# An S5 block and an SLN attention on one Trainium2 core: the closing layernorm split into halves, its product with g on GpSimd, later key loads, and seam values by way of ScalarE

## The chip, the cores and the metric

The kernel runs on one core of one Trainium2 chip. The metric is the device time of one launch in microseconds (us). The core has five engines that run their own instruction streams in program order: TensorE (PE, matrix products; PEld is its weight load), VectorE (DVE), ScalarE (ACT), GpSimd (POOL) and SyncE (SP, which here issues every DMA transfer). Engines wait for each other on semaphores.

## The reference

The input is x of shape (2, 2048, 512) and a condition vector per batch element. A first part, the S5 block, is a layernorm, a linear recurrence over time, and a gated feed-forward with GELU. Its output `hidden` goes through attention with a conditioned layernorm (SLN) on both sides:

```python
def _sln(h, w, ln_g, ln_b, Wg, bg, Wb, bb):
    mu = jnp.mean(h, axis=-1, keepdims=True)
    var = jnp.mean((h - mu) ** 2, axis=-1, keepdims=True)
    ln = (h - mu) / jnp.sqrt(var + EPS) * ln_g + ln_b
    gamma = (w @ Wg.T + bg)[:, None, :]
    beta = (w @ Wb.T + bb)[:, None, :]
    return gamma * ln + beta
h = _sln(hidden, w, ln_g, ln_b, Wg, bg, Wb, bb)
qkv = (h @ Wqkv.T + bqkv).reshape(B, N, num_heads, hd, 3)
...
att = jax.nn.softmax(energy, axis=-1) / D ** 0.5
out = jnp.einsum('bhqk,bhkd->bhqd', att, v)
...
out = out @ Wp.T + bp
h1 = out + hidden
h2 = _sln(h1, w, ln_g, ln_b, Wg, bg, Wb, bb)
return h2 + h1
```

There are 16 heads of 32, and every query sees all 2048 keys. The change lies in the last two lines (the second SLN, called the last norm below), in when keys and values are loaded, and in how some of the values v are written.

## The kernel before, in words

**Stages.** From 0 to 1380 us the S5 block and the feed-forward run in chunks of 512 tokens. The seam, to 1487 us, is where the last chunk's norm, features, heads and values (`at_norm`, `at_features`, `at_heads`, `at_values`) alternate with the first steps of attention. Attention runs to 3514 us, and the last four tiles are closed by `end_last` at 3551 us.

**Blocks and periods.** Attention is 64 blocks, one for each batch element b, pair of heads p and chunk c of 512 queries; batch element 0 has blocks 0 to 31, batch element 1 has 32 to 63. A block lasts 8 periods, called p0 to p7 here. The main loop (`for j in range(FIRST, NP * N + 2)`) writes one period after another, and an engine runs its instructions in the order written. Two blocks are under way in each period: for the block 15 periods ahead (AHEAD) scores and maxima are computed, for the block of now the exponentials and the weighted sum.

**One period, in the order written.** First `run_due(j)` issues what the dictionary `due` holds for j: loads, transposes, closing steps. Then, for the block of now, `make` (L812) computes a score tile again: PE writes `s` (L751), DVE adds the shift and writes `pT` (L816). For the block ahead, `across` (L769) has PE compute `m` (L776) and DVE reduce it to `top` (L781). `exponentials` on ACT (L821) follows. `keep` (L758) has PE compute a score tile, ACT copy it into a ring (L762) and DVE take the running maximum `run` (L767). Then comes the period's second exponential, `take_off` on POOL (L810, score minus maximum, for the next period) and `weighted` on PE (L831, o). Of 16 key tiles, ten are kept and six made anew.

**From the maxima to the shift.** `turn_run` (L783) transposes the running maximum on PE into the bank `pt_run` (L787) and DVE reduces it (L788); it comes twice, at a block's p2 for the one head and p4 for the other. `spread` at p5 transposes the result (`pt_neg`), copies it on ACT, and sends it through DRAM: SP writes `flat` (L802) and reads it back broadcast as `shift` (L804), 512 KB. POOL's `take_off` of the block waits for `shift`.

**One PSUM bank for many.** The scores `s` have two buffers of two banks, `m` two banks, `o` one. The bank with the tag "pt" is shared by `pt_run`, `pt_neg`, the projection `py`, the norm's `dev` and `z`: each has to wait until the one before it was read for the last time.

**Loads.** `load_k` reads 8 x 256 KB for the pair that opens at block n, every fourth block, and is due at period 8n - 27, which is p5 of block n - 4, ahead of that period's `spread`. `load_q` (8 transfers) is due at p3, `load_v` at 8n - 9, but not before OPEN, four periods ahead of block 0.

**Closing.** The 16 query tiles of batch element 0 are closed in blocks 34 to 56, those of the first three chunks of batch element 1 (12 tiles) in blocks 60 to 63. For a tile of batch element 0, with k at a block's p3: `fetch` at k (L874: the sums' quotients `by`, o and the residual `xr`), `divide` on POOL at k + 2, `project` in four matmuls at k + 3 to k + 6 (p6, p7, p0, p1) with `moments` (L909, DVE) right behind the last one, `deviation` (L917, eleven small DVE operations, the inverse root by Newton steps) at k + 7 (p2), `last_norm` at k + 8 (p3: ACT writes `z`, L941; DVE multiplies it by g, L943) and `close` at k + 9 (p4: two adds on POOL, L949 and L950, and the store). All of these are run by `run_due` at the start of their period.

Of the kernel before, what the change touches and what calls it, by code (L numbers as in the profile page):

```python
# [19 lines left out]
P = 128  # L20
# [19 lines left out]
def tile_s5_block_then_sln_attention(  # L40
# [497 lines left out]
        nc.sync.dma_start(dst[0, g * P : (g + 1) * P, at], hi.bitcast(F32))  # L538
        nc.sync.dma_start(dst[1, g * P : (g + 1) * P, at], lo.bitcast(F32))

    def at_values(b, c, t):
        pv = ones.tile([P, CH], F32, name="pv")
        for k in range(KC):
            nc.tensor.matmul(
                pv, fts[b, c][:, k, t * P : (t + 1) * P], wv[:, k, :], start=k == 0, stop=k == KC - 1
            )
        vt = work1.tile([P, D], F32, name="vt", tag="gated")
        nc.vector.tensor_add(vt, pv, bv_row)
        nc.sync.dma_start(vd[b][c * CH + t * P : c * CH + (t + 1) * P, :], vt)


# [129 lines left out]
    left = []  # L681
    for chunk in order[-2:]:
        for t in range(TT):
            left.append((at_values, *chunk, t))
    for j in range(2 * KC):
        left.insert(TT + j, (at_heads, *order[-1], j))
    for k in range(KC):
# [131 lines left out]
    def exponentials(n, kt):  # L819
        x = kept.pop((n, kt))  # L820
        nc.scalar.activation(x, x, AF.Exp)  # L821
        probs[n, kt] = x
# [71 lines left out]
    def project(b, qt, groups=tuple(range(NG))):  # L894

        o4, h, *py = held[b, qt]
        if py:
            py = py[0]
        elif len(groups) == NG:
            py = ps.tile([P, 2, CH], F32, name="py2", tag="m")[:, 0, :]  # L900
        else:
            py = ps.tile([P, CH], F32, name="py", tag="pt")
        for g in groups:
            nc.tensor.matmul(py, o4[:, g, :], wp[:, g, :], start=g == 0, stop=g == NG - 1)
        held[b, qt] = o4, h, py
        if groups[-1] == NG - 1:
            held[b, qt] = h, moments(h, py)

    def moments(h, py):  # L909
        nc.vector.tensor_add(h, py, h)  # L910
        st = small.tile([P, 6], F32, name="st3")
        nc.vector.bn_stats(st, h)
        mv = small.tile([P, 2], F32, name="mv3", bufs=4)
        nc.vector.bn_aggr(mv, st)
        return mv

    def deviation(b, qt):  # L917

        h, mv = held[b, qt]
        w = ps.tile([P, 3], F32, name="dev", tag="pt")  # L920
        v, c = w[:, 0:1], w[:, 1:2]
        half = small.tile([P, 1], F32, name="half3")
        y = small.tile([P, 1], F32, name="scale3", bufs=3)
        nc.vector.tensor_scalar(v, mv[:, 1:2], EPS, None, ALU.add)
        nc.vector.tensor_scalar(half, v, -0.5, None, ALU.mult)
        nc.vector.tensor_scalar(
            y.bitcast(I32), v.bitcast(I32), -0.5, float(0x5F3759DF), ALU.mult, ALU.add
        )
        for _ in range(3):
            nc.vector.tensor_scalar(c, y, y, half, ALU.mult, ALU.mult)  # L930
            nc.vector.scalar_tensor_tensor(y, c, 1.5, y, ALU.add, ALU.mult)
        shift = small.tile([P, 1], F32, name="shift3", bufs=3)
        nc.vector.tensor_scalar(c, mv[:, 0:1], y, None, ALU.mult)
        nc.vector.tensor_scalar(shift, c, -1.0, None, ALU.mult)
        held[b, qt] = h, y, shift

    def last_norm(b, qt):

        h, scale, shift = held[b, qt]
        z = ps.tile([P, CH], F32, name="z", tag="pt")  # L940
        nc.scalar.activation(z, h, AF.Identity, bias=shift, scale=scale)  # L941
        y = work.tile([P, D], F32, name="y")
        nc.vector.tensor_tensor(y, z, ending[b][0], ALU.mult)  # L943
        held[b, qt] = h, y

    def close(b, qt):

        h, y = held.pop((b, qt))
        nc.gpsimd.tensor_tensor(h, h, ending[b][1], ALU.add)  # L949
        nc.gpsimd.tensor_tensor(y, y, h, ALU.add)  # L950
        nc.sync.dma_start(out[b, qt * P : (qt + 1) * P, :], y)


# [98 lines left out]
    due = {}  # L1052

    def after(j, what, *args):
        due.setdefault(j, []).append((what, args))

    N = len(blocks)
    FIRST = -AHEAD - 8
    OPEN = -4
    for i, n in enumerate(opens):  # L1060
        free = NP * (max(m for m in range(N) if pair_of[m] == i - 2) + 1) if i > 1 else FIRST
        after(max(free, NP * n - AHEAD - 12), load_k, i)
        after(max(OPEN, NP * n - 9), load_v, i)
    for n in range(N):
        after(max(FIRST + 1 + n, NP * n - AHEAD - 6), load_q, n)
        after(NP * n - AHEAD + NP + 1, turn_run, n, 0)
# [2 lines left out]
    for b in range(NB):  # L1069
        for c in range(NQ):  # L1070
            j = NP * (blocks.index((b, NPAIR - 1, c)) + 1) + 1
            if (b, c) == (LB, LC):
                most = slice(0, NH - 4)
                j = NP * (N - 1) - 2
                after(j - 3, fetch_sums, b, c, most)
                after(j - 1, invert, b, c, most)
                after(j + 1, end_fetch)
                after(NP * (N - 1) + 3, end_fetch_more)
                for g in range(NG - 1):
                    after(j + 5 + g, end_divide, g)  # L1080
                after(NP * N + 2, end_project, list(range(NG - 1)))
                after(NP * N + 20, end_last)
                continue
            after(j, fetch_sums, b, c)
            after(j + 2, invert, b, c)
            if c == 0:
                after(j + 2, last_rows, b) if b == LB else after(NP * (NPAIR * NQ * (b + 1) + 2), last_rows, b)
            for t in range(TT):
                qt = c * TT + t
                if b == LB:  # L1090
                    k = j + 3 + 2 * t
                    after(k + 3, project, b, qt)
                else:

                    k = NP * (NPAIR * NQ * (b + 1) + 2 + 3 * qt // 2) + 3
                    for g in range(NG):
                        after(k + 3 + g, project, b, qt, (g,))
                last = k + 3 if b == LB else k + 6
                after(k, fetch, b, qt)
                after(k + 2, divide, b, qt)  # L1100
                after(last + 1, deviation, b, qt)
                after(last + 2, last_norm, b, qt)
                after(last + 3, close, b, qt)

    def run_due(j):
        for what, args in due.pop(j, ()):
# [6 lines left out]
    for j in range(FIRST, NP * N + 2):  # L1113
        if j == OPEN:
            assert not left
            late.close()
            fixed = ctx.enter_context(tc.tile_pool(name="fixed", bufs=1))
            kpools.append(ctx.enter_context(tc.tile_pool(name="kpool1", bufs=2)))
            ppool = ctx.enter_context(tc.tile_pool(name="ppool", bufs=2))
            rows = ctx.enter_context(tc.tile_pool(name="rows", bufs=2))  # L1120
            work = ctx.enter_context(tc.tile_pool(name="work2", bufs=2))
            ps_o = ctx.enter_context(tc.tile_pool(name="ps_o", bufs=1, space=PSUM))
            vst = [fixed.tile([P, NKT, 3, HD], F32, name=f"v{i}") for i in range(2)]
            for v in vst:
                nc.gpsimd.memset(v[:, :, 1, :], 1.0)
            wp = fixed.tile([P, KC, D], F32, name="wp")
        if j == 2:
            nc.sync.dma_start(wp, w_pT.rearrange("(k p) f -> p k f", p=P))
        if j == NP:
            nc.gpsimd.tensor_scalar(wp, wp, ISQ, None, ALU.mult)  # L1130
        run_due(j)
        n, i = block_at(j + AHEAD)
        todo = list(keeps[i]) if n is not None else []
        now, k = block_at(j)
        if now is not None and uses[k][1] >= NX:
            make(now, uses[k][1])
        if n is not None:
            across(n, i // TT, i % TT)
        if now is not None:
            exponentials(now, uses[k][0])  # L1140
        for kt in todo:
            keep(n, kt)
        if j == -AHEAD - 1:
            at_norm(*order[-1])
            pieces = TT
        elif -AHEAD <= j < -AHEAD + 2:
            pieces = 2
        elif j >= -AHEAD + 2:
            pieces = -(-len(left) // (OPEN - j)) if j < OPEN else 0
        else:  # L1150
            pieces = 0
        for _ in range(pieces):
            what, *args = left.pop(0)
            what(*args)
        if now is not None:
            exponentials(now, uses[k][1])
        n, i = block_at(j + 1)
        if n is not None:
            for kt in uses[i]:
                if kt < NX:  # L1160
                    take_off(n, kt)
        n, i = block_at(j - 1)
        if n is not None:
            for h, kt in enumerate(uses[i]):
                weighted(n, kt, i == 0 and h == 0, i == NP - 1 and h == 1)
# [56 lines left out]
```

## Time and profile before

| what | value |
|---|---|
| three runs | 3552.72, 3557.34, 3565.15 us |
| their median | 3557.34 us |
| the profiled execution | 3553.08 us |
| its span in the profile | 3551.2 us |
| PE, DVE, ACT, POOL busy | 95%, 63%, 53%, 56% |
| mean granted PE clock | 0.984 |
| DMA | 237.07 MB, mean 67 GB/s |

A row of groups names the line, engine, operation and tiles, then busy time, the mean ns of one, and the idle time of the engine just before, with what ended it. In the table of windows each engine has its busy time in a stretch, and PEclk is the share of full clock that PE was granted in it. A timeline gives start, duration, engine, line and, in square brackets, the wait that ended there. Periods and blocks are no fields of the trace: a block's start is that of its first exponential.

### The profile page before, as it was taken

What the parts mean: (1) busy time and instruction counts of PE and PEld (TensorE: products, weight loads), DVE (VectorE), ACT (ScalarE), POOL (GpSimd) and SP (SyncE); (2) the same over time, 40 slices, a digit from 0 to 9 for tenths busy, and PEclk for the clock granted to TensorE, in tenths of its full rate; (3) what the DMA queues carried; (4) which work ended last, traced back from release to release, by engine and by line L of the source; (5) the groups of instructions that cost most, each with busy time, mean ns of one, the idle gap of its engine ahead of it and who ended that gap; (6) DMA issues with size and microseconds to landing.
All of it is one profiled execution on the core that took longest, in us unless ns stands there. A gap on an engine that the chain in (4) does not pass through costs nothing. (4 is left out here: it accounts for less than half of the span.)

```text
span 3551.2 us, 34223 instructions
## 1 busy us (share of the span) xinstructions
PE 3375.1 (95%) x11752; PEld 1531.9 (43%) x11752; DVE 2243.7 (63%) x3184; ACT 1897.9 (53%) x2143; POOL 1977.0 (56%) x1000
## 2 busy tenths in 40 slices
PE   7999999999999998899999999999999999999986
PEld 4444444444444443444444444444444444444432
DVE  6233232323222212589999999898888888988875
ACT  2111112111111111488888888888777877877853
POOL 4223131313131311288778888887777777777875
PEclk8999999999999999999999999999999999999998
DMA  8011111111101112412321222232323323323233
GB/s 296 1 36 39 45 42 48 36 48 36 54 33 39 36 45 74 119 47 64 76 69 49 71 65 70 49 75 61 87 67 81 82 69 77 76 72 88 59 94 98
DMA packets 201710, 237.07 MB, mean 67 GB/s; under 512 B 89857, under 2 KB 119041, under 8 KB 197441
## 3 DMA queue, kind: packets, MB, share of 16 engines
q1 hardware_dynamic: 201536, 234.89, 23.8%
q8 instruction: 93, 1.52, 0.2%
q14 instruction: 81, 0.66, 0.1%
HBM read 166.91 MB, written 67.76 MB: 66 GB/s over the span
## 5 line engine op out<-in xcount | busy, mean ns | idle before, releaser
L810 POOL TENSOR_TENSOR x<-x,shift 128x1024 f32<-128x1024 f32 x640 | 1505.1, 2391 | 284.1 <-DMA shift<-flat 237.6
L762 ACT COPY x<-s 128x1024 f32<-128x1024 f32 x640 | 635.2, 1013 | 297.7 <-PE s L751 294.2
L751 PE MATMUL s<-qs,ks 128*128 128x512 f32 x2048 | 699.5, 433 | 78.0 <-DVE run L767 55.9
L821 ACT ACTIVATE x<-x 128x1024 f32<-128x1024 f32 x640 | 676.4, 1057 | 42.8 <-POOL x L810 42.7
L767 DVE TENSOR_TENSOR run<-s,run 128x1024 f32<-128x1024 f32 x512 | 625.2, 1221 | 76.3 <-ACT x L762 57.4
L831 PE MATMUL o<-x,v 128*64 128x512 f32 x2560 | 669.5, 618 | 0.9 <-ACT x L821 0.9
L816 DVE TENSOR_TENSOR pT<-s,shift 128x1024 f32<-128x1024 f32 x384 | 467.4, 1217 | 49.8 <-PE s L751 44.2
L781 DVE TENSOR_REDUCE top<-m 128x1 f32<-128x768 f32 x512 | 485.9, 949 | 19.6 <-PE m L776 19.2
L751 PEld LDWEIGHTS s<-qs,ks 128*128 128x128 f32 x2048 | 347.4, 190 | 333.3 <-DVE run L767 144.7
L502 PE MATMUL po<-w_sb,hid 128*128 128x512 f32 x1024 | 460.3, 592 | 0.0
L489 PE MATMUL ph<-fT,w_sb 128*128 128x512 f32 x1024 | 459.7, 593 | 0.0
L821 ACT ACTIVATE pT<-pT 128x1024 f32<-128x1024 f32 x384 | 407.5, 1061 | 76.6 <-DVE pT L816 63.2
L493 ACT ACTIVATE hid<-ph,vec 128x512 f32<-128x512 f32 x128 | 88.0, 687 | 591.4 <-PE ph L489 591.4
L831 PE MATMUL o<-pT,v 128*64 128x512 f32 x1536 | 397.3, 596 | 4.6 <-ACT pT L821 4.6
L160 DVE SCALAR_TENSOR_TENSOR lo<-pk,vec,hi 128x512 fp32r<-128x512 f32 x64 | 48.0, 751 | 501.5 <-ACT hi L159 501.5
L776 PE MATMUL m<-ks,qs 128*128 128x384 f32 x1024 | 288.0, 362 | 7.0 <-DVE top L781 3.3
L489 PEld LDWEIGHTS ph<-fT,w_sb 128*128 128x128 f32 x1024 | 191.8, 190 | 226.5 <-issue 226.5
L502 PEld LDWEIGHTS po<-w_sb,hid 128*128 128x128 f32 x1024 | 191.1, 190 | 221.5 <-issue 221.5
L436 POOL TENSOR_TENSOR m<-m,m 128x512 f32<-128x512 f32 x8 | 13.1, 1643 | 442.1 <-DVE m L434 442.1
L159 ACT ACTIVATE hi<-pk,vec 128x512 fp32r<-128x512 f32 x64 | 44.0, 688 | 391.9 <-PE pk L532 391.9
L831 PEld LDWEIGHTS o<-x,v 128*64 128x64 f32 x2560 | 139.5, 136 | 263.6 <-issue 157.9
L512 POOL TENSOR_TENSOR x<-x,gated 128x512 f32<-128x512 f32 x32 | 39.6, 1271 | 349.5 <-DVE gated L511 349.5
(236 smaller groups left out, 2825.1 us busy)
## 6 DMA issues: line engine op xcount, KB each, us to landing
ks<-kd SPq DMA_DIRECT2D x128, 256.0 KB
qs<-qd SPq DMA_DIRECT2D x512, 64.0 KB
shift<-flat SPq DMA_DIRECT2D x64, 512.0 KB
x<-in_x SPq DMA_DIRECT2D x8, 1024.0 KB
w_sb<-in_w SPq DMA_DIRECT2D x8, 1024.0 KB
x<-x SPq DMA_DIRECT2D x8, 1024.0 KB
kd<-hi SPq DMA_DIRECT2D x32, 256.0 KB
kd<-lo SPq DMA_DIRECT2D x32, 256.0 KB
```

Source lines behind the costliest of these rows:

```text
L489: nc.tensor.matmul(ph, w1_sb[:, k, f * P : (f + 1) * P], fts[b, c][:, k, :], start=k == 0, stop=k == KC - 1)
L493: nc.scalar.activation(hids[f], ph, AF.Gelu_apprx_tanh, bias=vec[:, V_B1 + f : V_B1 + f + 1], scale=1.0)
L502: nc.tensor.matmul(pos[b, c][:, t, :], hid[:, t * P : (t + 1) * P], w2_sb[:, f, :], start=f == 0, stop=f == FC - 1,)
L751: nc.tensor.matmul(s[:, e, :], kst[pair_of[n], e][:, kt * P : (kt + 1) * P], qst[n][:, e, :], start=True, stop=True,)
L762: nc.scalar.copy(x, s)
L767: nc.vector.tensor_tensor(runs[n], s, kept[n, 0] if kt == 1 else runs[n], ALU.max)
L776: nc.tensor.matmul(m[:, i, :YW], qst[n][:, e, t * P : (t + 1) * P], kst[pair_of[n], e][:, k : k + YW], start=True, stop=True,)
L781: nc.vector.tensor_reduce(tops[n][:, j, 0:1], m[:, :, :YW], AX.XY, ALU.max, negate=True)
L810: nc.gpsimd.tensor_tensor(x, x, shifts[n], ALU.add)
L816: nc.vector.tensor_tensor(x, s, shifts[n], ALU.add)
L821: nc.scalar.activation(x, x, AF.Exp)
L831: nc.tensor.matmul(outs[n][64 * e : 64 * e + 64, :], v[:, kt, e : e + 2, :], x[:, e, :], start=first, stop=final,)
```

## The change

**The last norm.** `moments` becomes a step of its own. A second kind of due time, `closing(j)`, is entered at j + 0.5 and issued after the exponentials of the period and before its `take_off` and `weighted`. For batch element 0, `moments` goes to the end of p1; `deviation` is cut in two, part 0 (five operations) at the end of p2 and part 1 (six) at the end of p3; `add_t` on POOL, h + t into the tile of o that is spent, goes to p3; `last_norm` to p5, its ACT operation writes `y` in SBUF and no `z` in PSUM; `close` goes to p6, where POOL multiplies `y` by g and adds h + t. The DVE product with g is gone. For the 12 tiles of batch element 1, both parts of `deviation` stand at one period's end, and `last_norm` and `close` (now three POOL operations) two periods behind it.

**Loads.** `load_k` is due at 8n - 22, p2 of block n - 3: behind `spread` of the block before and directly ahead of p3's `load_q` and `fetch`. The first `load_v` is due two periods later, at OPEN + 2.

**Values at the seam.** For the last chunk but one (four tiles), ACT copies `pv` from PSUM into `vt` and POOL adds the bias row, in place of one DVE addition.

```diff
--- before.py
+++ after.py
@@ -538,14 +538,18 @@
         nc.sync.dma_start(dst[0, g * P : (g + 1) * P, at], hi.bitcast(F32))
         nc.sync.dma_start(dst[1, g * P : (g + 1) * P, at], lo.bitcast(F32))
 
-    def at_values(b, c, t):
+    def at_values(b, c, t, beside_norm=False):
         pv = ones.tile([P, CH], F32, name="pv")
         for k in range(KC):
             nc.tensor.matmul(
                 pv, fts[b, c][:, k, t * P : (t + 1) * P], wv[:, k, :], start=k == 0, stop=k == KC - 1
             )
         vt = work1.tile([P, D], F32, name="vt", tag="gated")
-        nc.vector.tensor_add(vt, pv, bv_row)
+        if beside_norm:
+            nc.scalar.copy(vt, pv)
+            nc.gpsimd.tensor_tensor(vt, vt, bv_row, ALU.add)
+        else:
+            nc.vector.tensor_add(vt, pv, bv_row)
         nc.sync.dma_start(vd[b][c * CH + t * P : c * CH + (t + 1) * P, :], vt)
 
 
@@ -681,7 +685,7 @@
     left = []
     for chunk in order[-2:]:
         for t in range(TT):
-            left.append((at_values, *chunk, t))
+            left.append((at_values, *chunk, t, chunk != order[-1]))
     for j in range(2 * KC):
         left.insert(TT + j, (at_heads, *order[-1], j))
     for k in range(KC):
@@ -903,51 +907,63 @@
         for g in groups:
             nc.tensor.matmul(py, o4[:, g, :], wp[:, g, :], start=g == 0, stop=g == NG - 1)
         held[b, qt] = o4, h, py
-        if groups[-1] == NG - 1:
-            held[b, qt] = h, moments(h, py)
-
-    def moments(h, py):
+
+    def moments(b, qt):
+
+        o4, h, py = held[b, qt]
         nc.vector.tensor_add(h, py, h)
         st = small.tile([P, 6], F32, name="st3")
         nc.vector.bn_stats(st, h)
         mv = small.tile([P, 2], F32, name="mv3", bufs=4)
         nc.vector.bn_aggr(mv, st)
-        return mv
-
-    def deviation(b, qt):
-
-        h, mv = held[b, qt]
-        w = ps.tile([P, 3], F32, name="dev", tag="pt")
-        v, c = w[:, 0:1], w[:, 1:2]
-        half = small.tile([P, 1], F32, name="half3")
-        y = small.tile([P, 1], F32, name="scale3", bufs=3)
-        nc.vector.tensor_scalar(v, mv[:, 1:2], EPS, None, ALU.add)
-        nc.vector.tensor_scalar(half, v, -0.5, None, ALU.mult)
-        nc.vector.tensor_scalar(
-            y.bitcast(I32), v.bitcast(I32), -0.5, float(0x5F3759DF), ALU.mult, ALU.add
-        )
-        for _ in range(3):
+        held[b, qt] = h, o4.rearrange("p g q -> p (g q)"), mv
+
+    def add_t(b, qt):
+        h, ht, *_ = held[b, qt]
+        nc.gpsimd.tensor_tensor(ht, h, ending[b][1], ALU.add)
+
+    def deviation(b, qt, part):
+
+        h, ht, mv, *w = held[b, qt]
+        if part == 0:
+            dev = ps.tile([P, 3], F32, name="dev", tag="pt")
+            half = small.tile([P, 1], F32, name="half3")
+            y = small.tile([P, 1], F32, name="scale3", bufs=3)
+            v = dev[:, 0:1]
+            nc.vector.tensor_scalar(v, mv[:, 1:2], EPS, None, ALU.add)
+            nc.vector.tensor_scalar(half, v, -0.5, None, ALU.mult)
+            nc.vector.tensor_scalar(
+                y.bitcast(I32), v.bitcast(I32), -0.5, float(0x5F3759DF), ALU.mult, ALU.add
+            )
+        else:
+            dev, half, y = w
+        c = dev[:, 1:2]
+        for _ in range(1 + part):
             nc.vector.tensor_scalar(c, y, y, half, ALU.mult, ALU.mult)
             nc.vector.scalar_tensor_tensor(y, c, 1.5, y, ALU.add, ALU.mult)
-        shift = small.tile([P, 1], F32, name="shift3", bufs=3)
-        nc.vector.tensor_scalar(c, mv[:, 0:1], y, None, ALU.mult)
-        nc.vector.tensor_scalar(shift, c, -1.0, None, ALU.mult)
-        held[b, qt] = h, y, shift
+        if part == 0:
+            held[b, qt] = h, ht, mv, dev, half, y
+        else:
+            shift = small.tile([P, 1], F32, name="shift3", bufs=3)
+            nc.vector.tensor_scalar(c, mv[:, 0:1], y, None, ALU.mult)
+            nc.vector.tensor_scalar(shift, c, -1.0, None, ALU.mult)
+            held[b, qt] = h, ht, y, shift
 
     def last_norm(b, qt):
 
-        h, scale, shift = held[b, qt]
-        z = ps.tile([P, CH], F32, name="z", tag="pt")
-        nc.scalar.activation(z, h, AF.Identity, bias=shift, scale=scale)
+        h, ht, scale, shift = held[b, qt]
         y = work.tile([P, D], F32, name="y")
-        nc.vector.tensor_tensor(y, z, ending[b][0], ALU.mult)
-        held[b, qt] = h, y
+        nc.scalar.activation(y, h, AF.Identity, bias=shift, scale=scale)
+        held[b, qt] = h, ht, y
 
     def close(b, qt):
 
-        h, y = held.pop((b, qt))
-        nc.gpsimd.tensor_tensor(h, h, ending[b][1], ALU.add)
-        nc.gpsimd.tensor_tensor(y, y, h, ALU.add)
+        h, ht, y = held.pop((b, qt))
+        if b == LB:
+            ht = h
+            nc.gpsimd.tensor_tensor(h, h, ending[b][1], ALU.add)
+        nc.gpsimd.tensor_tensor(y, y, ending[b][0], ALU.mult)
+        nc.gpsimd.tensor_tensor(y, y, ht, ALU.add)
         nc.sync.dma_start(out[b, qt * P : (qt + 1) * P, :], y)
 
 
@@ -1052,15 +1068,20 @@
     due = {}
 
     def after(j, what, *args):
+
         due.setdefault(j, []).append((what, args))
+
+    def closing(j, what, *args):
+
+        due.setdefault(j + 0.5, []).append((what, args))
 
     N = len(blocks)
     FIRST = -AHEAD - 8
     OPEN = -4
     for i, n in enumerate(opens):
         free = NP * (max(m for m in range(N) if pair_of[m] == i - 2) + 1) if i > 1 else FIRST
-        after(max(free, NP * n - AHEAD - 12), load_k, i)
-        after(max(OPEN, NP * n - 9), load_v, i)
+        after(max(free, NP * n - AHEAD - 7) if i > 1 else max(FIRST, NP * n - AHEAD - 7), load_k, i)
+        after(max(OPEN + 2, NP * n - 9), load_v, i)
     for n in range(N):
         after(max(FIRST + 1 + n, NP * n - AHEAD - 6), load_q, n)
         after(NP * n - AHEAD + NP + 1, turn_run, n, 0)
@@ -1090,17 +1111,22 @@
                 if b == LB:
                     k = j + 3 + 2 * t
                     after(k + 3, project, b, qt)
+                    after(k + 3, moments, b, qt)
                 else:
 
                     k = NP * (NPAIR * NQ * (b + 1) + 2 + 3 * qt // 2) + 3
                     for g in range(NG):
                         after(k + 3 + g, project, b, qt, (g,))
+                    closing(k + 6, moments, b, qt)
                 last = k + 3 if b == LB else k + 6
                 after(k, fetch, b, qt)
                 after(k + 2, divide, b, qt)
-                after(last + 1, deviation, b, qt)
-                after(last + 2, last_norm, b, qt)
-                after(last + 3, close, b, qt)
+                closing(last + 1, deviation, b, qt, 0)
+                closing(last + (1 if b == LB else 2), deviation, b, qt, 1)
+                after(last + (3 if b == LB else 4), last_norm, b, qt)
+                after(last + (3 if b == LB else 5), close, b, qt)
+                if b != LB:
+                    after(last + 2, add_t, b, qt)
 
     def run_due(j):
         for what, args in due.pop(j, ()):
@@ -1154,6 +1180,7 @@
             what(*args)
         if now is not None:
             exponentials(now, uses[k][1])
+        run_due(j + 0.5)
         n, i = block_at(j + 1)
         if n is not None:
             for kt in uses[i]:
```

## The prediction

> **What bounds the kernel now.** I read the page's busy shares first, then the windows, the groups, the waits, and last the timelines around each stop. The page:
>
> ```profile
> PE 3375.1 (95%) x11752; PEld 1531.9 (43%) x11752; DVE 2243.7 (63%) x3184; ACT 1897.9 (53%) x2143; POOL 1977.0 (56%) x1000
> ```
>
> PE is the bound, so time is lost only where PE stands still or runs at half clock. The windows say where (PE busy is the second figure, then PEld, DVE, ACT, POOL, the clock):
>
> ```profile
> 1800.00:2000.00 200.00, 196.33 (x843) 89.59 (x843) 182.00 (x182) 178.45 (x195) 161.52 (x70) 1.00 0.29 69
> 2443.50:3284.00 840.50, 785.42 (x3173) 350.11 (x3171) 718.11 (x891) 661.64 (x719) 651.66 (x300) 0.98 0.31 75
> ```
>
> With nothing closing, a block lasts 28.79 us with PE busy 98%. The second window is blocks 33 to 57, which hold all 16 closings of batch element 0: 840.5 against 25 x 28.79 = 719.8, so 120.7 too much. I laid the block starts (first exponentials) side by side: 16 closings cost 5.40 each (86.4; of it 3.4 is PE's own projection, eight `py` matmuls at about 0.43, and 2.0 waiting); six blocks that load keys lose 25.0 (3.30, 5.68, 5.0, 2.86, 3.49, 4.70); `last_rows` 3.4 and half-clock stretches make the rest. The closing of block 36 on DVE and PE:
>
> ```profile
> 2554.86 0.69 DVE L788 TENSOR_REDUCE top<-pt_run 128x4 f32<-128x512 f32 x1
> 2555.59 0.16 DVE L924 TENSOR_SCALAR dev<-mv 128x1 f32<-128x1 f32 x1
> ...
> 2557.83 0.16 DVE L934 TENSOR_SCALAR shift<-dev 128x1 f32<-128x1 f32 x1
> 2557.90 1.22 DVE L816 TENSOR_TENSOR pT<-s,shift 128x1024 f32<-128x1024 f32 x1
> ...
> 2561.03 0.68 DVE L943 TENSOR_TENSOR y<-z,g_row 128x512 f32<-128x512 f32 x1
> ```
> ```profile
> 2559.17 0.72 PE L751 MATMUL s<-qs,ks 128*128 128x512 f32 x2 [1.21 <-DVE pT L816]
> 2560.04 0.62 PE L776 MATMUL m<-ks,qs 128*128 128x384 f32 x2
> 2561.17 0.73 PE L751 MATMUL s<-qs,ks 128*128 128x512 f32 x2 [0.51 <-DVE run L767]
> ```
>
> DVE has no gap from 2554.86 to p4; the 2.4 us of `deviation` hold up `pT`, and PE stands 1.21 + 0.14 + 0.51 = 1.86. The key load ahead of block 37 is the other stop:
>
> ```profile
> 2564.03 3.68 SPq L729 DMA_DIRECT2D ks<-kd  x8
> 2568.26 0.27 SPq L802 DMA_DIRECT2D flat<-neg_row  x1
> 2576.05 0.34 SPq L804 DMA_DIRECT2D shift<-flat  x1
> ```
> ```profile
> 2580.40 11.66 POOL L810 TENSOR_TENSOR x<-x,shift 128x1024 f32<-128x1024 f32 x5 [9.75 <-DMA shift<-flat]
> ```
> ```profile
> 2586.05 0.73 PE L751 MATMUL s<-qs,ks 128*128 128x512 f32 x2 [4.38 <-DVE run L767]
> ```
>
> `flat` was issued behind the keys, whose packets keep all queues busy to 2575 (10.4 us); `shift` could go only at 2576.05; POOL waited 9.75 and PE 4.38.
>
> [...] 4 KB of `flat` took from 2568.26 to about 2576. [...] a window only partly idle is enough: 1.96 of 3.41 busy, and half clock in the next:
>
> ```profile
> 2521.89:2525.30 3.41, 1.96 (x8) 0.59 (x4) 3.31 (x6) 1.61 (x2) 0.23 (x1) 1.00 0.59 114
> 2525.30:2528.71 3.41, 3.00 (x8) 1.12 (x10) 3.41 (x5) 2.80 (x4) 3.13 (x3) 0.51 0.46 48
> ```
>
> Each such piece costs about 1.4 (1.27 to 1.47 over those blocks). [...]
>
> **The change, part by part.** The sum is made on the profiled execution: 3553.08 (span 3551.2, the rest around it), 4.3 below the median of runs 3557.34. I add the differences to the median.
>
> *Last norm, 16 tiles.* DVE loses the product, 0.68 each. What remains is moved, and what decides is the spacing from the first `pt_run` (p2) to the second (p4): 7.10 without a closing, 9.53 with one in 11 of 16 cases of before. The bank "pt" is the reason to look there: `dev` lives in it until part 1 is done, and part 1 now stands behind p3's `run`, so the second `pt_run` waits for all DVE work of p2 and p3. That is `pt_run` itself until `top` starts, 0.69, then without a gap 0.69 + 2 x (1.22 + 0.95 + 1.22) less overlaps of starts = 7.02 in a plain block, part 0 (five operations to 2556.55 from 2555.59, 0.97) and part 1 (six, 1.48): 10.16 at least, against 9.53. So +0.63, x16 = +10.1. Moving `moments` behind p1's `pT` and `top` keeps the DVE total; `xr`, for which the first `pt_run` waits, ends about 2554.1 by my count, where it started at 2554.16: nothing, or 0.3 (then 3.45 in all against 2.43 of before: +1.02, +16.3). From below: DVE top of p4 came at 2564.75 anyway, so DVE was the late one already and PE may win its 0.63 back: 0.
>
> *Half clock.* Before, 5 of 16 closings had a piece. Now PE's idle, 1.86 + 0.63 = 2.5 to 3.1, is less scattered: most of it in one piece at p4. Idle of 1.45 in a window sufficed above. [...] I take 11 of 16: 6 x 1.4 = +8.5. Bounds 0 and +15.5 (all 16).
>
> *POOL and ACT there.* POOL gets y x g, 1.28 a tile, 20.5 in a window where it is busy 651.66 of 840.5; and it no longer stands waiting for `z`:
>
> ```profile
> POOL xr L949 <- ACT z L941: 63.5, 16, 5.3
> ```
>
> So it is hidden by POOL's lead in `take_off`; without that lead it would be 20.5. ACT's operation only moves from p3 to p5.
>
> *Keys.* Behind `flat` and `shift`, the six stops go: 25.0 less one half-clock piece of 1.4 in block 45 = -23.6. But eight key transfers, 3.68 of issue and 10.4 of packets, now stand ahead of `load_q` and `fetch` at p3 in the same SP queue, in blocks 33, 37, 41, 45, 49, 53, 57; `fetch` comes in 37, 41, 49 and 53. `load_q` has six periods, so no harm. For `by` the margin is thin: in block 40, with no keys ahead, it already lets POOL wait
>
> ```profile
> 2700.97 1.29 POOL L891 TENSOR_TENSOR o<-o,by 128x512 f32<-128x512 f32 x1 [5.83 <-DMA by<-invd]
> ```
>
> and `py` starts 2703.15, 0.9 after o is ready. With 10.4 of packets from p2, of which one period (3.6) passes before p3 and 0.9 is margin, less about 1.4 of overlap, 4.5 is left, and a half-clock piece, 1.3. I take it in two blocks (37 and 49) where the loads' completion order holds `by` up fully, and nothing in the others: +11.6. Bounds: 0, and four blocks, +23.
>
> *Seam.* PE stands 11.09 for the first `vt` (DVE has the norm before it) and 0.78 three times. ACT is idle there; but the third `vt` needs POOL's addition and a store that lands about 1402, so most of the wait returns as another: -2 (0 to -4). *First values* behind `flat`: their issue takes 1.93 and packets to 1483.3 ahead of `shift`, for which PE stood 4.07: -2.5 (0 to -4). *Last 12 tiles:* deviation hides beside `py` (-5), `pt_neg` near 3493 waits for it (+3.9), POOL's third operation at the end without a gap in its row (+3.3), the rest -3: -1 (-5 to +4).
>
> Sum: 10.1 + 8.5 - 23.6 + 11.6 - 2 - 2.5 - 1 = +1.1: **3558.4**.
>
> **Rivals.** *Absorbed:* DVE is the late engine at p4 in both kernels, so the longer wait of PE is repaid: the first two terms are nothing, 3558.4 - 18.6 = 3539.8, faster. For it: DVE has less work in all, 10.9 over the 16. Against: the next wait of PE after `pt_run` in block 36 is only 0.24. *Slower, the bank:* the second `pt_run` waits at its full length and in one piece, so each of 16 closings has 1.02 more and a half-clock piece: 16.3 + 15.5 = 31.8 in place of 18.6, 3571.6. [...] *Late `by`:* all four meetings of keys and `fetch` stop PE, +11.6 more: 3570. That the order of DVE is not as said is excluded: the instruction order of the changed kernel has part 1 behind p3's `run`, ahead of the second `pt_run`'s `top`.
>
> **How the numbers follow.** About 0.3% (10.7 us) is what can be told from no change: the three runs lie 12.4 apart. Forecast 0.42; absorbed 0.30; bank 0.18; late `by` 0.10. The first is "same", the second faster (below 3546.7), the last two slower (above 3568.0). Likeliest case alone: 3548 to 3567. The range takes in absorbed with no late `by` in half, about 3534, and the bank with the upper end of the small terms, 3580.
>
> **What would show it.** In the profile after: the weight load or matmul of the second `pt_run` waiting for DVE `shift3`, about 2 us, 16 times; spacing 10.2; more pieces of half clock in blocks 34 to 56; POOL's waits for `shift` down from 85.7 to under 30; waits for `by` up in blocks 37 and 49; no waits for z. The forecast is wrong if `pt_run` doesn't wait, if the closings cost under 5.0 a tile, or if `by` lands in time behind the keys.

## The result, and the profile after

| | median of runs | ratio to before, 95% interval |
|---|---|---|
| before | 3555.45 us (four runs) | |
| changed | 3608.12 us (3605.71 to 3610.03) | 1.0143 [1.0121, 1.0164] |

The change makes the kernel 53 us slower, where 1 us was forecast. The part up to the feed-forward's end has the same work in all kernels here, but its last matmul starts anywhere from 1379.1 to 1385.4 us in 14 profiles; for differences of a few us I therefore give stretches of the profiles beside the medians. Of the page after, the busy shares; PE is busy 11 us longer than before for the same matmuls, at a mean granted clock of 0.978 against 0.984, which suggests that more of them run at half clock:

```profile
PE 3385.9 (94%) x11752; PEld 1544.7 (43%) x11752; DVE 2224.1 (62%) x3152; ACT 1896.1 (53%) x2147; POOL 2015.9 (56%) x1032
```

To see where the time went I cut both spans at the starts of blocks. My count, here and in the prediction, took the loading of ACT's table (on the exponentials' line; 1.28 us, from 1487.4 before and 1486.2 after) for the first exponential, so every later cut lies at the last exponential of the block before:

| stretch of the profiled span, us | before | changed | difference |
|---|---|---|---|
| to block 0 | 1487.4 | 1486.2 | -1.2 |
| blocks 0 to 32 | 956.2 | 953.9 | -2.3 |
| blocks 33 to 57 | 840.5 | 851.7 | +11.2 |
| blocks 58 and 59 | 57.6 | 57.6 | 0 |
| block 60 to the end | 209.6 | 254.4 | +44.8 |

Cut at the first exponentials themselves, the differences are -3.2, -2.5, +13.5, 0 and +44.8, because the waits for `shift` ahead of blocks 0 and 33 then fall into the stretch before.

So 45 of the 53 us are in the last four blocks with the ending, where the 12 tiles of batch element 1 close. One of these tiles opens every two periods: with `fetch` at k, `divide` is due at k + 2, `project` and `moments` at k + 3, and `close` at k + 6, in the period of the `divide` of the second tile after it; `last_norm` was due at k + 5 and is due at k + 6 now. The windows of that stretch, before and then after (PE, PEld, DVE, ACT, POOL, clock):

```profile
3341.60:3551.20 209.60, 164.93 (x567) 65.75 (x563) 141.06 (x293) 101.28 (x114) 144.93 (x82) 0.93 0.33 95
```
```profile
3349.40:3603.80 254.40, 182.04 (x567) 72.05 (x563) 133.77 (x281) 101.03 (x114) 159.12 (x94) 0.86 0.27 78
```

POOL has 12 operations and 14 us more, but is busy only 63% of the stretch; nothing is busy all the time. PE has the same 567 matmuls, 17 us longer, at clock 0.86. An engine that is nowhere the bound, and a slower stretch: that is a chain of waits. The waits of this stretch after:

```profile
DVE xr L914 <- PE py L908: 77.6, 11, 11.5
POOL xr L964 <- ACT y L956: 57.9, 12, 9.8
...
ACT pT L825 <- DVE pT L820: 38.2, 8, 6.5
PE py L908 <- POOL o L895: 32.0, 8, 4.8
```

and of before:

```profile
DVE xr L910 <- PE py L904: 24.4, 10, 7.2
...
POOL xr L949 <- ACT z L941: 15.3, 6, 5.9
...
PE py L904 <- POOL o L891: 6.7, 3, 5.1
```

They close into a ring: PE's projection waits for POOL, POOL for ACT, ACT for DVE, and DVE for PE. One turn of it in the timelines after, PE, DVE, ACT and POOL:

```profile
3479.51 6.54 PE L908 MATMUL py<-wp,o 128*128 128x512 f32 x8 [3.46 <-POOL o L895]
...
3496.27 1.22 PE L908 MATMUL py<-wp,o 128*128 128x512 f32 x1 [4.75 <-POOL o L895]
```
```profile
3486.15 0.69 DVE L914 TENSOR_TENSOR xr<-py,xr 128x512 f32<-128x512 f32 x1 [10.51 <-PE py L908]
...
3488.14 2.29 DVE L820 TENSOR_TENSOR pT<-s,shift 128x1024 f32<-128x1024 f32 x2
```
```profile
3489.33 1.06 ACT L825 ACTIVATE pT<-pT 128x1024 f32<-128x1024 f32 x1 [6.47 <-DVE pT L820]
3490.29 0.80 ACT L956 ACTIVATE y<-xr,shift,scale 128x512 f32<-128x512 f32 x1
```
```profile
3491.16 1.27 POOL L964 TENSOR_TENSOR xr<-xr,t_row 128x512 f32<-128x512 f32 x1 [7.09 <-ACT y L956]
3492.41 1.25 POOL L965 TENSOR_TENSOR y<-y,g_row 128x512 f32<-128x512 f32 x1
3493.74 1.26 POOL L966 TENSOR_TENSOR y<-y,xr 128x512 f32<-128x512 f32 x1
3494.95 1.26 POOL L895 TENSOR_TENSOR o<-o,by 128x512 f32<-128x512 f32 x1
```

The projection `py` of one tile ends about 3486; DVE's `moments` of it stand ahead of the period's `pT`; ACT's exponential waits for that `pT`, and the `y` of the tile before stands behind the exponential; POOL's `close` of that tile waits for `y`; behind `close` stands the `divide` of the next tile (o, L895), and for that the next `py` waits. This turn takes 16.8 us. From one projection to the next it is 11.1 to 17.5 us in this stretch, and 8.8 to 14.7 in the kernel before. After the wait PE runs at half clock (0.50 from 3478.4 to 3485.2): `py` takes 6.54 here, and 3.70 at full clock.

In blocks 33 to 57 the two things that I had named are both there: the wait of the second `pt_run` and the keys ahead of `fetch`. The second `pt_run` waits for part 1 (PE and DVE of block 39, DVE without a gap to 2664.3):

```profile
2664.39 0.66 PE L791 MATMUL pt_run<-ident,run 128*128 128x128 f32 x4 [2.71 <-DVE shift L949]
```
```profile
2661.78 1.21 DVE L771 TENSOR_TENSOR run<-s,run 128x1024 f32<-128x1024 f32 x1
...
2664.17 0.16 DVE L949 TENSOR_SCALAR shift<-dev 128x1 f32<-128x1 f32 x1
```

And the keys stand ahead of `fetch`. SP's queue and PE in block 37:

```profile
2578.72 4.22 SPq L733 DMA_DIRECT2D ks<-kd  x8
2583.05 8.13 SPq L743 DMA_DIRECT2D qs<-qd  x8
...
2591.69 1.93 SPq L886 DMA_DIRECT2D by<-invd  x4
```
```profile
2601.22 2.07 PE L908 MATMUL py<-wp,o 128*128 128x512 f32 x2 [6.22 <-POOL o L895]
```

The eight issues of `load_q` took 8.13 us, and 3.62 in block 40 of the kernel before, with no keys ahead: six of the eight waited for the landing of a transfer of keys, 5.4 us in all. PE stood 6.22 for the `by` that came after them. The waits for `shift`, 85.7 us of POOL before, are 7.1 in these blocks, and the waits for `by` went from 38.6 to 93.5.

### The profile page after: what moved, and what is told of

The parts are those of the page before. It is cut to its first block, busy times and chain, and to the rows that moved or that the text cites. A ratio compares the mean times of both kernels' runs of the same rounds, so it can differ in the third digit from the quotient of the medians.

```text
span 3603.9 us, 34184 instructions
## 1 busy us (share of the span) xinstructions
PE 3385.9 (94%) x11752; PEld 1544.7 (43%) x11752; DVE 2224.1 (62%) x3152; ACT 1896.1 (53%) x2147; POOL 2015.9 (56%) x1032
## 3 DMA queue, kind: packets, MB, share of 16 engines
q1 hardware_dynamic: 201536, 234.89, 23.6%
q8 instruction: 93, 1.52, 0.2%
## 4 chain that ended last, share of the span: by engine, by line
PE 69%; DVE 15%; ACT 7%; issue 3%; DMA 3%; POOL 2%; SPq 1%; DVEq 0%; ACTq 0%; POOLq 0%
PE o L835 14%; PE ph L489 12%; PE po L502 12%; PE s L755 9%; DVE run L771 8%; PE pk L532 6%; ACT x L766 3%; PE py L908 3%; PE pv L544 3%; PE m L780 3%; DVE pT L820 2%; PE pt_run L791 2%; ACT pT L825 2%; PE pu L423 2%; DVE top L785 1%
```

## The experiments

Each was compared with the kernel before on the same chip. A line number is that of the kernel that the line is from. The tail runs have the changed kernel as their base.

**The tail: which part of the closing?**

```diff
-                after(last + (3 if b == LB else 4), last_norm, b, qt)
+                after(last + (2 if b == LB else 4), last_norm, b, qt)
```

> The changed kernel with one edit: for the 12 tiles of batch element 1, last_norm is due one period earlier, as before, so it is no longer in the period of its close. Loop theory: POOL's close waits for ACT's y, y stands behind exponentials that wait for DVE behind the next tile's moments, and the divide of the tile after stands behind close; a py every 16 us instead of every 9 to 13. With y a period earlier close doesn't wait: py spacing in blocks 62 and 63 falls from 15 to 17 us to about 11 to 12, and of the 44.8 us that blocks 60 to 63 with the tail have gained, 25 to 35 go: about 3575 to 3583. Rival, GpSimd's third operation alone: POOL is simply the bound there, the order doesn't matter, under 10 go: 3598 to 3608.

Measured: 3567.04 us, 1.0030 [1.0021, 1.0038]. 41 us are gone with one digit changed, more than expected; block 60 to the end takes 211.3.

```diff
         nc.scalar.activation(y, h, AF.Identity, bias=shift, scale=scale)
+        if b == LB:
+            nc.vector.tensor_tensor(y, y, ending[b][0], ALU.mult)
...
-        nc.gpsimd.tensor_tensor(y, y, ending[b][0], ALU.mult)
+        if b != LB:
+            nc.gpsimd.tensor_tensor(y, y, ending[b][0], ALU.mult)
```

> The changed kernel with one edit: for the 12 tiles of batch element 1, DVE multiplies y by g right after ACT's operation, in the same period as now, and close has two POOL operations. Loop theory: the loop stays, one POOL operation of 1.27 leaves it and a DVE operation of 0.68 with a wait enters: at most 0.6 to 1.3 a tile, 7 to 15 less: 3593 to 3601. Rival, the third operation alone: 30 or more go, under 3578.

Measured: 3599.0, 1.0115 [1.0100, 1.0130]. 9 us less: one POOL operation left the ring, a shorter DVE operation came in, and the ring stays. The third POOL operation alone is not the cause.

```diff
-                closing(last + 1, deviation, b, qt, 0)
-                closing(last + (1 if b == LB else 2), deviation, b, qt, 1)
-                after(last + (3 if b == LB else 4), last_norm, b, qt)
+                if b == LB:
+                    after(last + 1, deviation, b, qt, 0)
+                    after(last + 1, deviation, b, qt, 1)
+                else:
+                    closing(last + 1, deviation, b, qt, 0)
+                    closing(last + 2, deviation, b, qt, 1)
+                after(last + (2 if b == LB else 4), last_norm, b, qt)
```

with `z` in PSUM and the product with g on DVE for these tiles.

> The changed kernel with the 12 tiles of batch element 1 closed as before: deviation at the period's start, last_norm one period earlier into z in PSUM, the product with g on DVE. All theories that put the loss into these tiles' closing: blocks 60 to 63 with the tail go back to about 209.6 us from 254.4, so 3608 - 45 = 3563, within 4. If the loss came from something else that reaches into these blocks (the 8 us later start, keys, fetches), it stays above 3575.

Measured: 3561.95, 1.0015 [1.0008, 1.0022]; the end stretch takes 208.5. All of the 44.8 us belong to these tiles' closing. Between this and the first edit lie 5 us; they differ in g on POOL or DVE, in `z` in PSUM, and in `deviation` at a period's end or start, and no run separates these.

```diff
-                after(last + (3 if b == LB else 5), close, b, qt)
+                after(last + (4 if b == LB else 5), close, b, qt)
```

> The changed kernel with one edit: for the 12 tiles of batch element 1, close is due one period later than in the change; last_norm, deviation, moments and all three GpSimd operations stay. Loop theory: what costs is that close stands on GpSimd ahead of the divide of the tile two further while y isn't there yet; with close behind that divide, py no longer hangs on y, and 30 to 45 us go although no operation is taken away and ACT's order is the same: 3563 to 3578. Rival, the late place of last_norm on ACT itself (or the late deviation): the time stays above 3595.

Measured: 3566.6, 1.0031 [1.0018, 1.0044], 41.5 us less. This run settles it: no operation is taken away, ACT's order stays, only `close` stands behind the `divide` on POOL instead of ahead of it. POOL in it, then PE:

```profile
3470.33 1.29 POOL L895 TENSOR_TENSOR o<-o,by 128x512 f32<-128x512 f32 x1
3471.57 2.37 POOL L814 TENSOR_TENSOR x<-x,shift 128x1024 f32<-128x1024 f32 x1
3473.89 1.28 POOL L964 TENSOR_TENSOR xr<-xr,t_row 128x512 f32<-128x512 f32 x1
```
```profile
3462.76 3.60 PE L908 MATMUL py<-wp,o 128*128 128x512 f32 x8
...
3471.75 3.70 PE L908 MATMUL py<-wp,o 128*128 128x512 f32 x8
```

POOL has no wait in these lines, `py` follows `py` in 9.0 us, and at full clock. The ring is open, though single waits stay: over the whole stretch PE's `py` waits 8.7 us for POOL, and not 32.0, and POOL's `close` 13.3 for `y`, and not 57.9.

**The keys.** The kernel before with the change's load time alone:

```diff
-        after(max(free, NP * n - AHEAD - 12), load_k, i)
+        after(max(free, NP * n - AHEAD - 7) if i > 1 else max(FIRST, NP * n - AHEAD - 7), load_k, i)
```

> The kernel before with one edit: load_k at 8n - 22 as in the change (p2 of block n - 3, ahead of load_q and fetch). Theory: the move only exchanges stops. The six stops of POOL for shift (25 us of PE) go, and five stops for by come (blocks 37, 49 at p6, some 8 us each; 41, 53, 56 some 4 each: 28): within 8 us of before, 3550 to 3564. Rival, the prediction's: only two meetings cost, 11.6 against 23.6: 12 us faster, 3544.

Measured: 3558.75, 1.0009 [1.0001, 1.0016]: an exchange of stops. And with another time, - 11 in the place of the first - 7 (period 8n - 26, p6 of block n - 4):

> The kernel before with one edit: load_k at 8n - 26, p6 of block n - 4: one period behind spread's flat and shift, five periods ahead of load_q and fetch. Theory (the queue's order is what costs): both kinds of stop go, 20 to 26 us faster than before: 3530 to 3536. Rival: eight transfers of 256 KB in the way always cost something, shift's landing or the stores of sd and od: no more than 10 us faster.

Measured: 3530.84, 0.9934 [0.9919, 0.9949], 26 us faster. The keys' transfers alone cost nothing that shows here: block 36, where this run loads keys, takes 32.50 us, and block 39, without keys, 32.47. What costs is what stands behind them in the queue. In this run that is nothing urgent; `shift` is issued at 2570.92, ahead of the keys:

```profile
2569.68 0.27 SPq L802 DMA_DIRECT2D flat<-neg_row  x1
...
2571.31 4.90 SPq L729 DMA_DIRECT2D ks<-kd  x8
...
2585.61 3.61 SPq L739 DMA_DIRECT2D qs<-qd  x8
```

Block by block, the move to p2 costs 8.4 (block 37), 1.8 (41), 7.8 (49), 3.9 (53) and 5.9 (56) against p6: 27.8 of the 30.6 by which blocks 33 to 57 differ in the two profiles; the medians lie 27.9 apart.

**The halved norm.**

```diff
-            dev = ps.tile([P, 3], F32, name="dev", tag="pt")
+            dev = small.tile([P, 3], F32, name="dev", bufs=3)
```

> The changed kernel with one edit: dev is a small tile in SBUF, not in the PSUM bank that pt_run and the others share, so the second pt_run does not wait for part 1. Bank theory (the prediction's first two terms): the 16 closings of batch element 0 get 0.6 to 2 us shorter each and lose half-clock pieces, 10 to 30 us less: 3578 to 3598. Rival, DVE is late at that place anyway and PE only waits a little later: under 5 us less, 3603 to 3608, with PE's wait for shift3 turned into waits for DVE pT or run.

Measured: 3621.16, 1.0175 [1.0160, 1.0190]: 13 us slower than the change, which neither theory had. The second `pt_run` no longer waits for `deviation` (in block 39 it starts without a wait), but another thing came with the edit. One DVE operation, first in the changed kernel and then in this one (ns min/median/max):

```profile
L943 DVE SCALAR_TENSOR_TENSOR scale<-dev,scale x84: 157/157/160, 2517.8 to 3556.7; 128x1 f32<-128x1 f32 x84
```
```profile
L943 DVE SCALAR_TENSOR_TENSOR scale<-dev,scale x84: 159/842/6765, 2516.2 to 3571.8; 128x1 f32<-128x1 f32 x84
```

With all operands in SBUF, 48 of the 84 began while POOL was busy; they took 1.00 us in the median and up to 6.8, and 46 of them ended within 0.03 us of the end of a POOL instruction. The other 36 took 0.16. The run says nothing on the bank, then; it shows a cost that `dev` in PSUM avoids.

The two kernels that follow are the changed kernel with the tail as before and the keys at p6 (both edits are shown above), so that the norm is alone:

> The changed kernel with two edits: the 12 tiles of batch element 1 closed as before, load_k at 8n - 26. What stays of the change is the halved norm with g on POOL for 16 tiles, the seam values and the later first load_v. Theory: the tail gives back 46, the keys 25 or so: 3530 to 3540; it differs from the kernel before with keys at 8n - 26 by +7 (0.44 a closing) and +5 (half-clock pieces) less 3.3 (seam and first values), so up to 9 us slower than that one. Rival: the halved norm is worth something once the other stops are gone: faster than that one by 5 or more.

Measured: 3538.95, 0.9958 [0.9944, 0.9972].

```diff
-                if b == LB:
-                    after(last + 1, deviation, b, qt, 0)
-                    after(last + 1, deviation, b, qt, 1)
-                else:
-                    closing(last + 1, deviation, b, qt, 0)
-                    closing(last + 2, deviation, b, qt, 1)
+                for part in range(2):
+                    after(last + 1, deviation, b, qt, part)
```

> The kernel of the run before (tail as before, load_k at 8n - 26) with one more edit: for batch element 0 both parts of deviation stand at the start of p2, as before, so the second pt_run doesn't wait for them; moments at the end of p1, g on POOL at p6 stay. Bank theory: the wait of 2.7 at each second pt_run goes; DVE is 0.68 shorter in p2 and p3 than in the kernel before: 0.44 to 1.1 a closing better and half as many half-clock pieces, 10 to 20 us faster than the run before: 3515 to 3527. Rival, DVE backlog: the same DVE work in p2 and p3 makes PE wait elsewhere for as long: within 4 us of the run before.

Measured: 3535.06, 0.9949 [0.9933, 0.9966]: 4 us by the medians, the rival's number. The profiles say more: blocks 33 to 57 take 822.9 us, and 829.9 in the run before. The wait at the second `pt_run` is gone, and PE waits in p2, ahead of `pT`, as before. The next two are built on the kernel before with the keys at p6. Without the product with g for batch element 0:

```diff
-        z = ps.tile([P, CH], F32, name="z", tag="pt")
-        nc.scalar.activation(z, h, AF.Identity, bias=shift, scale=scale)
         y = work.tile([P, D], F32, name="y")
-        nc.vector.tensor_tensor(y, z, ending[b][0], ALU.mult)
+        if b == LB:
+            z = ps.tile([P, CH], F32, name="z", tag="pt")
+            nc.scalar.activation(z, h, AF.Identity, bias=shift, scale=scale)
+            nc.vector.tensor_tensor(y, z, ending[b][0], ALU.mult)
+        else:
+            nc.scalar.activation(y, h, AF.Identity, bias=shift, scale=scale)
```

> The kernel before with load_k at 8n - 26, and with the product with g left out for the 16 tiles of batch element 0 (ACT writes y to SBUF; the output lacks the factor g there): 16 DVE operations of 0.68 less, 10.9 us of DVE work, nothing else added. Theory: these stand in p3, where DVE has caught up, and hide behind PE: at most 3 us faster than the same kernel with the product, 3527 to 3532. Rival, the prediction's step (DVE work between the two pt_runs counts in full): 8 to 11 us faster, 3520 to 3523.

Measured: 3529.54, 0.9930 [0.9913, 0.9947], 1.3 us under the same kernel with the product; blocks 33 to 57 take 3.4 us less (813.9 and 817.3). Of the products' 10.9 us most was hidden; to take them off DVE could bring little. And, with g again, the seam values and the first `load_v` of the change added, word for word as in its diff:

> The kernel before with three edits: load_k at 8n - 26, and of the change the seam values by way of ScalarE and GpSimd and the first load_v two periods later. The norm, its product with g and the tail are as before. From the parts: 3530.8 (keys alone) less 2 to 4.5 for seam and first values: 3526 to 3529, about 28 us under the kernel before and the fastest of all. Rival: the seam's gain is taken back by the third vt's waits: the same as with keys alone, within 1.5 us.

Measured: 3527.42, 0.9921 [0.9907, 0.9936]. It differs from the 3538.95 us kernel by the norm of batch element 0 alone, as halved and moved, which so costs 11.5 us; 10.0 by blocks 33 to 57 (829.9 and 819.9). In these blocks PE waits 43.3 us for `deviation`'s `shift` and 7.2 for `run` with the halved norm, 19.1 for `pT` and 17.7 for `run` without it; with `deviation` whole at p2 (the 3535.06 us kernel) it is 20.5 and 17.4. So the wait at the second `pt_run` is most of that cost, 7.0 of the 10.0 by the stretch, though only 3.9 of the 11.5 by the medians. Against keys alone (3530.84) the seam and first values bring 3.4. The intervals overlap, but from the last matmul of the feed-forward to the cut ahead of block 33 four profiles without these two edits take 1063.0 to 1063.7 us, and ten with them 1059.5 to 1060.4.

**A version that beats both.** On the last kernel:

```diff
-                after(last + 1, deviation, b, qt)
-                after(last + 2, last_norm, b, qt)
-                after(last + 3, close, b, qt)
+                if b == LB:
+                    after(last + 1, deviation, b, qt)
+                else:
+                    for part in range(3):
+                        after(last + 5 + part + 0.5, spread_deviation, b, qt, part)
+                o = 0 if b == LB else NP
+                after(last + 2 + o, last_norm, b, qt)
+                after(last + 3 + o, close, b, qt)
...
+        nc.vector.tensor_scalar(c, y, y, half, ALU.mult, ALU.mult)
+        nc.vector.tensor_scalar(y, c, 1.5, y, ALU.add, ALU.mult)
```

`dev` is in SBUF, and `last_norm` and `close` come a block later; each of the three parts has one Newton step, the last one also the shift; half steps of time are run as in the change.

> The kernel before with load_k at 8n - 26, seam values and first load_v as in the change, and one more edit: for the 16 tiles of batch element 0 deviation is cut in three and moved to the ends of p6, p7 and p0, a block later than its projection, with dev in SBUF (so it holds no part of the shared bank) and with tensor_scalar in place of scalar_tensor_tensor; last_norm and close follow at p3 and p4 of that block, g on DVE as before. Theory: what a closing costs beside projection is PE waiting for DVE behind deviation in p2; in p6 to p0 PE has projections or DVE has slack, so of 2.0 us a closing 1 to 1.7 go (16 to 27 us) and some half-clock pieces with them: 3498 to 3512. Rival, the backlog only moves: DVE has 9% to spare in a plain block, so PE waits in p6 to p0 for as long: within 5 us of the same kernel without the edit, 3522 to 3532.

Measured: 3495.86 (3494.01 to 3497.49), 0.9823 [0.9808, 0.9839], 61 us faster than the kernel before and a little under the range expected. Blocks 33 to 57, in the kernel without the edit and then with it:

```profile
2440.00:3259.90 819.90, 780.08 (x3173) 347.75 (x3171) 717.92 (x891) 660.36 (x719) 649.55 (x299) 0.99 0.32 79
```
```profile
2444.80:3229.10 784.30, 768.81 (x3171) 344.77 (x3169) 711.55 (x884) 659.89 (x719) 646.33 (x297) 1.00 0.34 82
```

PE is now busy 98% there, and no piece at half clock is left in these blocks (seven without the edit). The 35.6 us of this stretch are 24.4 of PE's waits and 11.3 of its busy time for the same work: the 16 waits for `pT` in p2, 19.1 us, are gone. Three things were moved at once (the place of the steps, `dev` out of the bank, the form of the product), and no run separates them.

## Why the prediction was wrong, point by point

- **Last 12 tiles: forecast -1 (-5 to +4), measured +44.8.** This is the step that failed. I had summed single waits (deviation beside `py`, `pt_neg`, POOL's third operation, 3.3) and did not ask what stands behind `close` on POOL. There stands the `divide` of a later tile. With `last_norm` and `close` due in one period, POOL waits in `close` for an ACT operation that is queued behind exponentials of the period before, and the next projection waits for POOL. With `last_norm` one period earlier POOL waits for `y` in 4 of the 12 closings, 13.2 us, and not in 12, 57.9. The third operation, all that I priced of `close`, is 9 of the 45.
- **Keys: stops removed, forecast -23.6.** Right: with the keys out of everybody's way 26 are gained, 23.2 of them in blocks 33 to 57.
- **Keys: new meetings with `fetch`, forecast +11.6 (0 to 23), measured 27.9.** Mechanism right, size wrong, outside its own bounds. I counted two meetings that cost, 5.8 each; they cost 8.4 and 7.8, and three more that I had put at nothing cost 1.8, 3.9 and 5.9. I had put the last pair's load into block 57; that pair opens at block 59, so the load falls into block 56, where there is a `fetch`. I also counted 10.4 us of packets for the keys; in the profile before they run 10.0, from 2565.2 to 2575.2. And I left out that the issues of `load_q` wait for the keys' landing (8.13 against 3.62): that alone makes `by`, issued behind them, 4.5 later, an estimate from these two figures.
- **Second `pt_run`: forecast +10.1, and half-clock pieces +8.5.** Mechanism right: PE waits 43.3 us there in 16 closings, 2.7 each, in one piece. Mis-sized: the two `pt_run` are 9.95 us apart in all 16 closings, and not 10.2, so a closing without a half-clock piece is 0.43 longer than before (block 39: 32.90 against 32.47), not 0.63, and the term is +6.9. Of half-clock pieces blocks 33 to 57 have 11 with the halved norm, as forecast (the 11 of 16 was my estimate), but 7 without it (5 in the kernel with keys alone), so 4 to 6 more. Together 11.5 for 18.6. The rival *absorbed* is out: PE gets back only a part of the wait, in shorter waits for `run` (7.2 for 17.7).
- **Seam and first values: forecast -4.5**, measured -3.4 in a pair of runs, -3.5 in the stretches of the table. Right within what can be told. PE's 11.09 and two waits of 0.78 (the prediction has three) for `vt` became 1.77, 0.73 and 8.58: most of the wait came back at a later `vt`, as the prediction said.
- **Rival *late `by`*** was the nearest to what came in blocks 33 to 57: its +23.2 for all meetings, measured 27.9. With the tail as before the changed kernel stands at 3561.95, 3.5 us above the forecast and well inside its range. That is partly luck, since the two mis-sized terms (+16.3 and -7.1) partly cancel; the terms as measured add up to about +9.6, and the run says +5.8 against its own kernel before. The range was missed by the last 12 tiles alone.
- **The clock** is part of the tail's size: PE's busy time is 17 us longer for the same matmuls, and seven pieces of 6.83 us at half clock fall into the turns of the ring; with the ring open there are only four single pieces of 3.41 in its place. In the 3.41 us ahead of each of the seven pieces PE is busy for 0 to 1.49 us, and in only two of the seven cases it is idle throughout. The 1.96 of 3.41 busy ahead of the prediction's piece is one case of the profile before; in the profile after, from 1500 us on, 13 stretches of 3.41 at full clock with PE busy for 1.52 to 1.96 are followed by full clock.

What stays open: how much of the tail's 44.8 us is half clock and how much waiting. PE's busy time says 17 for the clock and its idle time 28 for the waits, but no run took one away without the other.

## What to carry to other kernels

When a step is moved next to its consumer in time, list what is queued behind the consumer on its engine, and follow that one to its own consumers; a ring through four engines shows in no engine's busy time, only in waits that name each other. A transfer that is moved in a queue can leave one victim for another: move it to where the longest stretch without an urgent transfer begins, and count the meetings from the actual schedule. Operations that hide are worth little when removed (16 products of 0.68 us: 1.3 us); operations that hold up the producer of what the bound engine waits for can be worth most of their length when they move into slack (16 times 2.4 us: 31.6 us, half clock included).

## What the runs showed of the hardware

Of the 84 DVE `scalar_tensor_tensor` on 128x1 with all operands in SBUF (the 3621.16 us kernel), 48 began while POOL was busy. Their median was 1.00 us, against 0.16 for the other 36: about six times as long, for an operation of a single column. Of the 48, 46 ended within 0.03 us of the end of a POOL instruction; the longest, 6.77 us, lasted through three in a row. With one operand in PSUM (the changed kernel), 57 of the 84 began while POOL was busy, and all took 0.16. A `tensor_scalar` with the second factor as its scalar does the same product; the last kernel uses it, and all 48 of these, which began while POOL was busy, took 0.21 each. Why the times differ, no run shows.
